# Down product of a 4-bit FFN: seven of eleven weight chunks as whole numbers in single passes

## Chip, cores, metric

The kernel runs on one core of one Trainium2 chip. The metric is the device time of one execution in microseconds; lower is better. A run of the kernel before is quoted by the median of three executions.

## The reference, cut to what matters

The program is four layers, each an attention and a feed-forward part (FFN). Only the first FFN (L0 FFN) is changed. It takes x of 4 x 256 = 1024 tokens by 512 features, three 4-bit weight matrices (gate and up 512 x 1376, down 1376 x 512), and computes down(silu(gate(x)) * up(x)). A weight is a whole number of 0 to 15 less a zero point, times a scale for each group of 128 input rows and each output column:

```python
def dequant_gptq(qweight, scales, zeros, groupsize):
    q = qweight[k // PACK, :] >> (k % PACK * 4)[:, None] & 15
    z = zeros[:, n // PACK] >> (n % PACK * 4)[None, :] & 15
    zp = (z.astype(jnp.float32) + 1.0) * s
    return q.astype(jnp.float32) * s[k // groupsize] - zp[k // groupsize]
```

So q - z - 1 is a whole number between -16 and 14, and within one group of 128 rows the scale can be taken out of the sum over rows. The 1376 rows of the down matrix are 11 chunks of 128 (the last one padded), and each chunk is exactly one group.

## The kernel before

All 1024 tokens are handled as 8 tiles of 128 (NT = 8), features as 4 chunks of 128 (NC = 4). Activations x_sb hold tokens on the partitions; xT holds features on the partitions. The order of every engine's instructions in the L0 FFN is the order in the source (`manual_schedule`); DMA instructions on SP's queue and everything outside this function are placed by the tile framework's scheduler. Each engine executes its own queue in order. Waits are set by the framework, by tile: an instruction waits for earlier users of the memory that it touches.

**Weights ahead of time.** `GateUp` (L596 on) works in the shadow of the attention: it fetches the packed words of gate and up, shifts out the nibbles (`nibble`), subtracts the zero points (`whole`, L666) and keeps whole numbers, for the first READY = 3 blocks as float32r and for eight more as float16. `points` (L620 on) forms the zero points of all three matrices; for down it forms scaled zero points and stores them to DRAM (`down_zp`).

**Gate and up** (`Sum`, L746 on; loop at L790). There are 22 sub-products: 11 blocks of 128 inner features, gate and up for each. x was split into a high half (float32r) and the rest (`hi`, `lo`), so that a product of x with whole-number weights takes two single-pass matmuls. Each sub-product is 4 groups x 2 token halves x 2 (hi, lo) = 16 matmuls into four PSUM tiles of two banks (F=4); ACT scales two of them out of PSUM (L776), DVE scales and adds the other two (L778), POOL adds the two sums (L783, `added`), ACT takes the Silu (L798) and DVE multiplies gate by up (L801) into hT, which holds inner features on the partitions: 11 chunks x 1024 tokens, float32. ACT also widens float16 weights to float32r (`widen`, L678).

**Down** (L816 on). `down_fetch` has SP fetch packed words, scales and scaled zero points of one chunk, mostly into xT, which is free by then; `down_weights` shifts the nibbles out on DVE (L718), multiplies by the scales on DVE (L722) and subtracts the scaled zero points on POOL (L723), giving float32 weights in `wd`. Chunks 0 and 1 are made during the last gate/up sub-products, the others during the product. `product` (L730) is one float32 matmul: 128 tokens of hT are the stationary side, the 512 weight columns move, and the result has tokens on the partitions. The loop first does chunks 0 to 4 for all eight token tiles, then chunks 5 to 10 for tiles 0 to 3; `output` copies the PSUM tile to float16 on ACT (L727) and adds it to x_sb on DVE (L728). While tiles 4 to 7 get chunks 5 to 10, layer 1's norm of tiles 0 to 3 runs in steps between them (statistics, L140 normalisation, L147 transposes, L906 queries).

**What lies around it.** `x2` is the pool that holds hi and lo; it is closed at L815, and layer 1's weights (`layer1_begun`: w1, rank, bqk, b1 by SP; gate_b and bv by POOL's queue) are loaded into its place. `values_binding` (L863 on) works on bv: seven DVE instructions (L867 to L852 of `signs`), a memset on POOL, and an ACT operation on bqk. `binding` needs that ACT result for a small matmul (L881). Layer 2's first weights (`Layer2Weights`, SP L91 and L1114, eight sums on POOL at L1095 and L1099) are loaded when the pools of the gate and up weights are given back, after the last `down_weights`. The `wd` buffer is also lent to the attention: output weights `wo` in chunks 0 to 3, attention outputs `oT` in chunks 4 to 9.

Of the kernel before, what the change touches and what calls it, by code (L numbers as in the profile page):

```python
# [23 lines left out]
I32 = mybir.dt.int32  # L24
# [16 lines left out]
ROWS = NBLK * P // PACK  # L41
READY = 3
# [13 lines left out]
def block_stack(ctx: ExitStack, tc: tile.TileContext, d: dict, out: bass.AP):  # L56
# [94 lines left out]
    def layer0_attention(hook, aside, xp, wd):  # L151
# [13 lines left out]
        with (  # L165
# [10 lines left out]
            wo = wd[:, 0:4, :]  # L176
# [82 lines left out]
            class Batch:  # L259


                def __init__(self, b):
# [3 lines left out]
                    k = 4 + 2 * (b % 3)  # L266
                    self.oT = wd[:, k : k + 2, :].rearrange("p c i -> p (c i)")
# [328 lines left out]
    class GateUp:  # L596
# [6 lines left out]
        def __init__(self, pool, raw, ready, held, dram):  # L603
            self.pool, self.raw, self.ready, self.held = pool, raw, ready, held
            self.built = {}

            self.z = dram.tile([2, 4, NBLK, P], F16, name="gu_z1")
            self.down_zp = dram.tile([NBLK, C], F32, name="down_zp")

        def load(self):  # L610
# [4 lines left out]
            ds = self.raw.tile([P, 4, P], F16, tag="z", name="ds_rows")  # L615
            self.ds = ds[0:NBLK].rearrange("p c i -> p (c i)")
            nc.sync.dma_start(out=self.ds, in_=d["down_s"])
            self.s = self.pool.tile([P, 2, NBLK, 4], F32, name="gu_s32")

        def points(self):  # L620
# [3 lines left out]
            dzi, zp = (self.raw.tile([P, 4, P], I32, tag="q", name=k) for k in ("d_zi", "d_zp"))  # L624
            dzi, zp = (x[0:NBLK].rearrange("p c i -> p (c i)") for x in (dzi, zp.bitcast(F32)))
# [8 lines left out]
            def finish():  # L634
# [4 lines left out]
                nc.vector.scalar_tensor_tensor(zp, dzi, 1.0, self.ds, ALU.add, ALU.mult)  # L639
                nc.sync.dma_start(out=self.down_zp, in_=zp)  # L640
# [3 lines left out]
        def pieces(self, blk):  # L644
            steps = []
            self.built[blk] = ws = []
            for m, name in enumerate(("gate", "up")):
# [13 lines left out]
                def whole(name=name, had=had):  # L661
                    if blk < READY:
                        w = self.ready.tile([P, 4, P], F32R, tag=name, name=f"{name}_w_{blk}")
                    else:
                        w = self.held.tile([P, 4, P], F16, name=f"{name}_h_{blk}")
# [15 lines left out]
    def layer0_ffn(gu, layer1_begun, x2, wd, hi, lo, outputs):  # L681
        E = mybir.EngineType
        with (
# [8 lines left out]
            spare = [xT[:, c, :].rearrange("p (k i) -> p k i", k=2) for c in range(NC)]  # L692
            fetched_down = {}

            def down_fetch(m, pool=None):

                if pool is not None:
                    q = pool.tile([P, C], I32, tag="dq", name=f"dq_{m}")
                    s = pool.tile([P, C], F16, tag="ds", name=f"ds_{m}")
                    zp = pool.tile([P, C], F32, tag="dzp", name=f"dzp_{m}")  # L700
                elif m != 6:
                    k = (m - 2) % 5
                    q, zp = spare[k][:, 0].bitcast(I32), spare[k][:, 1]
                    s = xT[:, NC - 1, k * 256 : (k + 1) * 256].bitcast(F16)
                else:
                    q = gu.raw.tile([P, 4, P], I32, tag="q", name=f"dq_{m}")
                    zp = gu.raw.tile([P, 4, P], F32, tag="q", name=f"dzp_{m}")
                    s = gu.raw.tile([P, 4, P], F16, tag="z", name=f"ds_{m}")
                    q, zp, s = (x.rearrange("p c i -> p (c i)") for x in (q, zp, s))
                nc.sync.dma_start(out=q, in_=bc(d["down_q"][:, m], 0, 8))  # L710
                nc.sync.dma_start(out=s, in_=bc(d["down_s"][m], 0, P))
                nc.sync.dma_start(out=zp, in_=bc(gu.down_zp[m], 0, P))
                fetched_down[m] = q, s, zp

            def down_weights(m):

                q, s, zp = fetched_down[m]
# [3 lines left out]
                w = wd[:, m, :]  # L721
                nc.vector.tensor_tensor(w, q, s, ALU.mult)  # L722
                nc.gpsimd.tensor_tensor(w, w, zp, ALU.subtract)  # L723
# [6 lines left out]
            def product(t, po, k):  # L730
# [3 lines left out]
                    rhs=wd[:, k, :],  # L734
                    start=k == 0,
                    stop=k == NBLK - 1,
                )

# [1536 lines left out]
```

## Time and profile before

| | us |
|---|---|
| median of 3 executions (lowest, highest) | 1412.58 (1407.13, 1414.27) |
| profiled execution, its own time | 1412.54 |
| span of the profiled execution | 1410.8 |
| first gate/up matmul | 275.27 |
| first and last down matmul (starts) | 369.35, 446.5 |
| first matmul of layer 1 (rank) | 447.80 |
| busy TensorE / DVE / ACT / POOL, share of span | 96% / 63% / 37% / 52% |

Times within the profile count from the start of the span. A matmul's record starts when it is issued, and the next begins before its end is reached; so the price of one in a row of many is the distance of starts, not the duration. The mean granted TensorE clock was 0.983 of full speed.

### The profile page before, as it was taken

The page shows a single profiled execution, that of the slowest core. Times are in us where ns is not written, and L with a number is a line of the kernel's source. Part 1 is how long each engine was busy: PE and PEld are TensorE (multiplying, and loading weights), DVE is VectorE, ACT ScalarE, POOL GpSimd, SP SyncE. Part 2 cuts the span into 40 slices and gives each one's busy share as a digit, 9 for nine tenths or more (in the row PEclk, how much of TensorE's full clock was granted, in tenths as well). Part 3 has the DMA queues.
Part 4 walks back from the last instruction along what each step waited for, and adds up shares of the span by engine and source line. Part 5 has one row for each costly group of instructions (what it writes and reads, how often), then busy time and mean ns, then how long its engine had stood idle before and what let it go on. Part 6 is the DMA issues. An engine that isn't in the chain of part 4 may idle for free.

```text
span 1410.8 us, 20812 instructions
## 1 busy us (share of the span) xinstructions
PE 1359.0 (96%) x7300; PEld 1068.8 (76%) x7300; DVE 895.8 (63%) x2366; ACT 520.7 (37%) x1337; POOL 734.1 (52%) x760
## 2 busy tenths in 40 slices
PE   7989999999999999999999999999999999989998
PEld 5656666578545667888888888888888888867887
DVE  6777878468927249635756756665566655858654
ACT  2343435378303212332333432333333344535430
POOL 3445546457743105864777857868558675210210
PEclk9889999899999999999999999999999999999999
DMA  5021212400420021011312203211123000302001
GB/s 195 2 58 35 47 35 63 111 0 1 140 80 16 0 80 48 31 46 34 98 45 64 68 16 94 68 46 64 53 60 105 22 25 1 135 1 112 0 1 60
DMA packets 50812, 76.15 MB, mean 54 GB/s; under 512 B 16476, under 2 KB 23799, under 8 KB 50323
## 3 DMA queue, kind: packets, MB, share of 16 engines
q1 hardware_dynamic: 49778, 73.77, 17.0%
q8 instruction: 58, 0.95, 0.3%
q10 hardware_dynamic: 816, 0.79, 0.2%
q14 instruction: 48, 0.39, 0.1%
q0 software_dynamic: 112, 0.26, 0.1%
HBM read 66.89 MB, written 7.91 MB: 53 GB/s over the span
## 4 chain that ended last, share of the span: by engine, by line
PE 84%; DVE 10%; ACT 2%; issue 1%; POOL 1%; DMA 1%; SPq 0%; DVEq 0%; ACTq 0%; POOLq 0%
PE m L1367 18%; PE m L1331 15%; PE dn L731 5%; PE gu L763 5%; PE s L1720 4%; PE av L1793 4%; PE m L1353 3%; PE m L1343 3%; PE half L278 3%; PE st L435 2%; PE s L1724 2%; PE av L1794 2%; PE l1o L1010 2%; DVE masked L389 2%; PE half L318 2%; PE half L343 1%
## 5 line engine op out<-in xcount | busy, mean ns | idle before, releaser
L1768 POOL TENSOR_TENSOR p<-p,rs 128x512 f32<-128x512 f32 (+1 forms) x128 | 107.7, 863 | 160.6 <-DVE rs L1765 148.9
L1754 ACT ACTIVATE p<-p,nm 128x256 f32<-128x256 f32 (+1 forms) x256 | 113.2, 443 | 108.2 <-DVE nm L1738 108.0
L1331 PE MATMUL m<-xT,wq_b 128*128 128x256 f32 x448 | 105.5, 384 | 4.4 <-DVE x_sb L1590 3.0
L1425 DVE TENSOR_TENSOR x_sb<-x_sb,m 128x512 f32<-128x512 f32 x82 | 55.9, 685 | 82.4 <-PE m L1367 67.4
L1738 DVE CUSTOM_DVE_ANT_0 p<-s,cmask 128x256 f32<-128x256 f32 (+1 forms) x256 | 76.1, 353 | 45.9 <-PE s L1720 43.8
L1391 POOL TENSOR_TENSOR q<-q,t 128x512 f32<-128x512 f32 x64 | 82.3, 1287 | 31.5 <-DVE t L1382 28.2
L389 DVE CUSTOM_DVE_ANT_0 masked<-s,cmask 128x256 f32<-128x256 f32 (+1 forms) x256 | 89.8, 351 | 11.7 <-PE s L376 2.0
L1802 ACT COPY o<-av 128x512 f32<-128x512 f32 x64 | 37.5, 586 | 157.7 <-PE av L1794 157.7
L1331 PEld LDWEIGHTS m<-xT,wq_b 128*128 128x128 f32 x448 | 83.2, 193 | 15.2 <-DVE x_sb L1590 3.4
L1314 POOL TENSOR_TENSOR c<-c,z 128x512 f32<-128x512 f32 x28 | 36.5, 1303 | 111.0 <-DVE c L1311 50.7
L449 POOL TENSOR_SCALAR_AFFINE_SELECT keys<-keys 128x256 f32<-128x256 f32 x128 | 57.0, 457 | 66.0 <-ACT keys L445 64.6
L1367 PE MATMUL m<-wo_b,o 128*128 128x256 f32 x384 | 89.6, 379 | 0.0
L1382 DVE TENSOR_TENSOR t<-m,rope_sb 64x512 f32<-64x512 f32 (+1 forms) x144 | 86.3, 599 | 2.1
L445 ACT ACTIVATE keys<-st 128x384 f32<-128x384 f32 x128 | 57.3, 488 | 78.1 <-PE st L435 78.1
L1786 ACT COPY q<-pT 128x512 f32<-128x512 f32 x64 | 37.5, 585 | 122.5 <-PE pT L1777 120.5
L731 PE MATMUL dn<-wd,hT 128*128 128x512 f32 x176 | 76.4, 593 | 2.3 <-DVE sb L778 2.3
L1367 PEld LDWEIGHTS m<-wo_b,o 128*128 128x128 f32 x384 | 71.3, 190 | 8.8
L783 POOL TENSOR_TENSOR sa<-sa,sb 128x1024 f32<-128x1024 f32 x22 | 62.0, 2822 | 30.5 <-DVE sb L778 30.5
L1331 PE MATMUL m<-x_s,wq_t 128*128 128x256 f32 x320 | 75.4, 380 | 1.2 <-ACT kv L1416 1.1
L1331 PEld LDWEIGHTS m<-x_s,wq_t 128*128 128x128 f32 x320 | 59.8, 190 | 10.1 <-ACT kv L1416 1.5
L1793 PE MATMUL av<-q,kv 128*128 128x512 f32 x128 | 65.5, 593 | 0.9 <-ACT q L1787 0.9
L1720 PE MATMUL s<-kv,q 128*128 128x256 f32 x256 | 65.8, 379 | 0.0
(328 smaller groups left out, 3423.8 us busy)
## 6 DMA issues: line engine op xcount, KB each, us to landing
wq_b<-in_wq SPq DMA_DIRECT2D x38, 256.0 KB
wo_b<-in_wo SPq DMA_DIRECT2D x32, 256.0 KB
raw<-in_wo SPq DMA_DIRECT2D x16, 512.0 KB
wkv_b<-in_wkv SPq DMA_DIRECT2D x16, 256.0 KB
wos_d<-wos_row SPq DMA_DIRECT2D x28, 128.0 KB
gate_q<-in_gate_q SPq DMA_DIRECT2D x11, 256.0 KB
up_q<-in_up_q SPq DMA_DIRECT2D x11, 256.0 KB
wq3s_b<-in_wq SPq DMA_DIRECT2D x8, 256.0 KB
```

Source lines behind the costliest of these rows:

```text
L389: nc.vector.tensor_tensor_reduce(out=ap.tile([P, T], F32, tag="masked", name="masked", bufs=1)[:, 0:n], in0=self.s[part][i][:, e, :], in1= ...
L731: nc.tensor.matmul(po, lhsT=hT[:, k, t * P : (t + 1) * P], rhs=wd[:, k, :], start=k == 0, stop=k == NBLK - 1,)
L763: nc.tensor.matmul(p[:, half], lhsT=w[:, g, :], rhs=x[half][:, g], start=k == 0, stop=k == 1,)
L1331: nc.tensor.matmul(out[:, i, :], lhsT=b[:, c, i * P : (i + 1) * P], rhs=a[:, c, :], start=start and i == 0 and c == 0, stop=i == 1 and c == 1,
L1367: nc.tensor.matmul(out[:, t, :], lhsT=a[:, c, t * P : (t + 1) * P], rhs=b[:, c, :], start=start and t == 0 and c == 0, stop=t == 1 and c = ...
L1382: nc.vector.tensor_tensor(t2[at], src[of], sin[of], ALU.mult)
L1391: after(1 + 2 * pause, lambda: nc.gpsimd.tensor_tensor(dst, dst, t2, ALU.add))
L1720: nc.tensor.matmul(s1[:, i, :], lhsT=q[:, i, P:T], rhs=kt[:, 0, :], start=True, stop=True)
L1738: nc.vector.tensor_tensor_reduce(out=x[f"p{part}"][:, e, :], in0=x[f"s{part}"][:, e, :], in1=cmask if part else cmask[:, P : 2 * P], scale ...
L1754: nc.scalar.activation(p, p, AF.Exp, bias=x["nm"][:, part, e : e + 1], scale=-1.0, accum_out=x["sums"][:, part, e : e + 1],)
L1768: nc.gpsimd.tensor_tensor(p, p, bc(x["rs"][:, part, :], 2, n), ALU.mult)
L1793: nc.tensor.matmul(av, lhsT=v[:, 0:P], rhs=x["q0"], start=True, stop=False)
```

## The change

The constant WHOLE = 7 divides the chunks of the down product.

Chunks 0 to 6 keep whole-number weights: `down_weights` shifts the nibbles out and subtracts the zero point (now q - (z + 1), float32r), and applies no scale. hT of these chunks is split into a float32r part (ACT) and the rest (POOL) by `split`. `whole` multiplies with the weights as the stationary side: 128 output columns on the partitions, 512 tokens moving, two token halves, two parts each, in single passes. A result (one chunk, 128 output columns, 1024 tokens) takes a PSUM tile of two banks; `scaled` multiplies it by the scale, which is now a value for each partition, and adds it to `acc` in SBUF: on DVE for three of four column blocks, and by ACT and POOL for the fourth. `turned_back` brings the sums into the output's layout with a float32 matmul against the identity, accumulating on top of the other chunks' result.

Chunks 7 to 10 stay as they were: scaled float32 weights (scale now multiplied on POOL) and `product`. Sixteen of these products (tiles 0 to 3) are placed before and between the 28 steps of the whole-number loop, the others in the second half as before.

Around this: PSUM is one pool of four two-bank tiles A to D through the whole FFN, and pairs of token tiles share one (dn_0 with dn_1, and so on); zero points of down are stored unscaled in DRAM and fetched in one broadcast; packed words of chunks 7 to 10 go straight into their weight buffers; `acc` takes the place of the float16 gate/up weights and the split parts take the places of gate/up weights (chunks 0 and 5) and of hi and lo (the others); x2 is closed after the loop, and `values_binding` follows it. The diff, cut to its core:

```diff
+WHOLE = 7
...
+            def down_tiles():
...
+                nc.sync.dma_start(out=points, in_=bc(gu.down_z1, 0, P))
+                nc.sync.dma_start(out=scales, in_=bc(d["down_s"][WHOLE:NBLK], 0, P))
+                for m in (0, 7, 1, 8, 9, 10):
+                    down_fetch(m)
...
             def down_weights(m):
-                q, s, zp = fetched_down[m]
+                w, q = wds[m], packed[m]
                 nc.vector.tensor_scalar(
                     q, q, gu.shift, 15, ALU.logical_shift_right, ALU.bitwise_and
                 )
-                w = wd[:, m, :]
-                nc.vector.tensor_tensor(w, q, s, ALU.mult)
-                nc.gpsimd.tensor_tensor(w, w, zp, ALU.subtract)
+                nc.vector.tensor_tensor(w, q, points[:, m, :], ALU.subtract)
+                if m >= WHOLE:
+                    nc.gpsimd.tensor_tensor(w, w, scales[:, m - WHOLE, :], ALU.mult)
+                elif m + 2 < WHOLE:
+                    down_fetch(m + 2)
+            def split(k, eng):
...
+                for i, h in enumerate(hs):
+                    nc.scalar.copy(x[2 * i], h)
+                for i, h in enumerate(hs):
+                    eng.tensor_tensor(x[2 * i + 1], h, x[2 * i].bitcast(F32), ALU.subtract)
+                halves[k] = x[:2], x[2:]
+            def whole(k, n, p):
+                for h in range(2):
+                    for i, x in enumerate(halves[k][h]):
+                        nc.tensor.matmul(
+                            p[:, h],
+                            lhsT=wds[k][:, n * P : (n + 1) * P],
+                            rhs=x,
+                            start=i == 0,
+                            stop=i == 1,
+                        )
+            def scaled(k, n, p):
+                s, a = gu.ds[:, n, k : k + 1], acc[:, n]
+                if k == 0 and n % 2 == 0:
+                    nc.scalar.activation(a, p, AF.Copy, scale=s)
+                elif k == 0:
+                    nc.vector.tensor_scalar(a, p, s, None, ALU.mult)
+                elif n == 3:
+                    part = once.tile([P, 2, 512], F32, tag="part", name=f"part_{k}")
+                    nc.scalar.activation(part, p, AF.Copy, scale=s)
+                    nc.gpsimd.tensor_tensor(a, a, part, ALU.add)
+                else:
+                    nc.vector.scalar_tensor_tensor(a, p, s, a, ALU.mult, ALU.add)
+            def turned_back(t, po):
+                for n in range(4):
+                    nc.tensor.matmul(
+                        po[:, n * P : (n + 1) * P],
+                        lhsT=acc[:, n, t // 4, t % 4 * P : (t % 4 + 1) * P],
+                        rhs=ident,
+                        start=False,
+                        stop=n == 3,
+                    )
...
+                    if u in (8, 12, 16, 20):
+                        down_weights({8: 0, 12: 7, 16: 1, 20: 8}[u])
+                    if u in (20, 21):
+                        split(u - 20, nc.gpsimd)
+                side = {
+                    2: [lambda: down_weights(2)],
+                    3: [lambda: split(2, nc.gpsimd)],
+                    4: [lambda: finish(len(subs) + 1)],
+                    5: [lambda: split(3, nc.gpsimd)],
+                    6: [lambda: down_weights(3)],
+                    8: [lambda: split(4, nc.gpsimd), lambda: down_weights(9)],
+                    11: [lambda: down_weights(4)],
+                    12: [lambda: split(5, nc.gpsimd)],
+                    14: [lambda: down_weights(10)],
+                    15: [lambda: down_weights(5)],
+                    17: [lambda: split(6, nc.gpsimd)],
+                    19: [lambda: down_weights(6)],
+                }
+                po = []
+                for _ in range(2):
+                    two = bank([P, 2, 512], f"dn_{len(po)}")
+                    po += [two[:, 0], two[:, 1]]
+                between = [(t, k) for k in range(WHOLE, NBLK) for t in range(4)]
+                for _ in range(4):
+                    t, k = between.pop(0)
+                    product(t, po[t], k)
+                finish(len(subs))
+                ring = turn[0] + 1
+                for i in range(4 * WHOLE):
+                    k, n = divmod(i, 4)
+                    p = ps("ABCD"[(ring + i % 2) % 4], [P, 2, 512], f"dw_{k}_{n}")
+                    whole(k, n, p)
+                    scaled(k, n, p)
+                    for f in side.get(i, ()):
+                        f()
+                    if i >= 4 and i % 2 == 0 and len(between) > 2:
+                        t, j = between.pop(0)
+                        product(t, po[t], j)
+                for t, k in between:
+                    product(t, po[t], k)
             x2.close()
-            ctx0.enter_context(psum_banks("ps_f1", F=4, G=4))
             l1 = layer1_begun()
-            po = [ps("FG"[t // 4], [P, C], f"dn_{t}") for t in range(NT)]
-            early, rest = range(NBLK // 2), range(NBLK // 2, NBLK)
-            for k in early:
-                if k >= 2:
-                    down_weights(k)
-                    down_fetch(k + 5)
-                for t in range(NT):
-                    product(t, po[t], k)
             l1.values_binding()
-            for k in rest:
...
             for t in range(4):
+                turned_back(t, po[t])
                 output(t, po[t])
-            steps = l1.norm(0, "F")
-            steps.insert(1, lambda: l1.binding("F"))
+            tags = ["ABCD"[(ring + i) % 4] for i in range(4)]
+            for i in range(2):
+                two = ps(tags[i], [P, 2, 512], f"dn_{len(po)}")
+                po += [two[:, 0], two[:, 1]]
+            steps = l1.norm(0, tags[2:])
+            steps.insert(1, lambda: l1.binding(tags[2]))
             for t in range(4, NT):
                 steps[t - 4]()
-                for k in rest:
+                for k in range(WHOLE, NBLK):
                     product(t, po[t], k)
+                turned_back(t, po[t])
                 output(t, po[t])
```

`finish(u)` holds what the gate/up loop did at L794 to L801 (the sum, the Silu, the multiplication of an earlier sub-product); its last two calls now stand in the down product.

## The prediction

> **What bounds the kernel now.** The mean clock is 0.983 and TensorE is busy for 96% of the span, so only a stretch in which TensorE does less, or waits, can move the time. First the chain of waits through the end of the feed-forward network, then busy time by stretch:
>
> ```profile
> 368.02 1.29 DVE sb L778
> 369.35 60.35 PE dn L731 x140
> 429.82 5.25 PE dn L731 x12
> 435.95 5.15 PE dn L731 x12
> 441.98 5.17 PE dn L731 x12
> 447.16 0.59 ACT o L727
> 447.80 3.80 PE rank L933 x32
> ...
> 288.00:367.00 79.00, 79.00 (x339) 62.96 (x337) 65.40 (x57) 64.50 (x69) 57.64 (x21) 1.00 0.04 9
> 367.00:447.00 80.00, 77.68 (x195) 35.24 (x194) 45.93 (x71) 8.12 (x13) 37.75 (x28) 1.00 0.29 89
> ```
>
> The columns of the last two are stretch, length, then busy time (instructions) of PE, PEld, DVE, ACT and POOL. The down product is a solid TensorE block with other engines half idle; gate and up before it are also TensorE-bound, at 3.74 us for one of 22 sub-products. I measure from the end of the last gate/up matmul (starts 366.64, takes 0.40: 367.04) to the first rank matmul (447.80): **80.76 us**. Prices, from the groups by line and by source:
>
> ```profile
> L731 PE MATMUL dn<-wd,hT x176: 592/592/697, 369.4 to 446.5; 128*128 128x512 f32 x176
> ...
> L783 POOL TENSOR_TENSOR sa<-sa,sb x22: 2341/2414/3381, 290.6 to 370.6; 128x1024 f32<-128x1024 f32 x22
> L778 DVE SCALAR_TENSOR_TENSOR sa<-gu,gu_s,sa x22: 1272/1284/1284, 288.0 to 366.8; 128x1024 f32<-128x1024 f32 x22
> L722 DVE TENSOR_TENSOR wd<-xT x6: 693/1636/1642, 375.6 to 392.6; 128x512 f32<-128x512 int32 x6
> L801 DVE TENSOR_TENSOR hT<-hT,sa x11: 1212/1216/2477, 301.7 to 373.9; 128x1024 f32<-128x1024 f32 x11
> bv<-in_bv POOLq DMA_DIRECT2D x1, 256.0 KB, 4.0
> ```
>
> Durations are minimum/median/maximum in ns. The 88 products of the source leave 176 records, 140 of them in 60.35 us: one product costs 2 x 0.431 = **0.862 us**. Gate/up matmuls (f32r) start every **0.2335 us** and leave one record. DVE's evacuation from PSUM starts every 1.20 us when queued; ACT's (L776) every 1.02.
>
> **What the Trainium skill says.** "FP8 and Floating Point Precision", TensorE Precision Notes: true FP32 makes four passes. The trace agrees: 0.862/0.2335 = 3.7. "SBUF — State Buffer", SBUF: two separate sides: a DVE operation with two SBUF inputs and a GpSimd one that reads SBUF exclude each other; the one that "starts first gets the pair for the whole instruction". The trace agrees: L722 takes 0.69 alone and 1.64 while L723 runs, L801 1.21 or 2.4, L783 2.41 or 3.33; L778, with one operand in PSUM, never varies. "DMA: Bandwidth & Descriptors", Anatomy of one DMA, fits a GpSimd-issued transfer at 2.0 us + bytes/436 KB per us: an estimate of 2.6 us for bv; the trace says 4.0, which I take, keeping 2.6 as the short end.
>
> **TensorE's own work.** Seven of eleven chunks leave the FP32 form: 7 x 8 x 0.862 = 48.3 us go. In come 7 chunks x 4 output blocks x 2 halves x 2 (high, low) = 112 single passes x 0.2335 = 26.2, and 8 x 4 turning matmuls of 128 columns at 0.22 (L1018: 8 records, 4 instructions, in 0.89) = 7.0. The change of PSUM pool at 366.6 to 369.35 goes too (2.3). Net -17.4 us, **if nothing waits**. Things wait.
>
> **The loop.** From 367.04, four FP32 products (chunk 7) run at once: 3.45. Then 28 steps of 0.934, ten products put between them (8.6): 34.8. All 28 steps share two two-bank buffers, so each waits for the evacuation two steps back, and DVE has other work between evacuations:
> - Start. POOL must first scale chunk 8 (1.3), split chunk 0 (2 x 1.24) and add sub-product 20 (2.36); it ends near 372.3. ACT stands at the Silu that needs this add (0.97), and the first evacuation is behind it. The third step starts near 374.5: a stall of 2.3, and 0.4 at the fifth.
> - The last hT multiply at step 4 (DVE, 2.3 with POOL ahead of it): 1.6 over two steps.
> - down_weights (0.5 + 0.62 alone, 1.55 beside POOL) at steps 2, 6, 8, 11, 14, 15, 19: 1.5 at step 8, 1.8 at the pair 14/15, 0.4 at 19, nothing where TensorE has a product to do.
> - Chunk 6 has no products between its steps: 0.934 against an evacuation of 1.28 gives about 1.0.
> Sum 9.0, and 0.1 for each of eleven restarts (first dn record after its idle time: 697 against 592 ns): 10.1. Loop: 3.45 + 34.8 + 10.1 = **48.3**, ending at 415.3 = T.
>
> DVE alone in it: 18 x 1.2 + 2 x 1.2 + 7 x 1.1 to 2.1 + 2.3 = 34 to 41. Bounds: no exclusion at all, loop 44.9 (-3.4); every exclusion against us, POOL at 1.4/2.8, loop 52.2 and 2.2 more in gate/up (+6).
>
> **The tail, where I expect the gain to go.** The split activations lie where layer 1's weights go, so w1, rank, bqk, gate_b and bv load only after the loop's last matmul (before: issued 368.7 to 375, under the product), and values_binding moves from the middle of the product to the front of the DVE queue after the loop. By the built order and its waits:
> - POOL: memset of lowT (1.2; before at 375.2), the last sum (2.4) to T+3.75, gate_b issue (0.7), bv issued at T+4.5, landed T+8.5.
> - DVE: values_binding, 4.4 us (380.38 to 384.80 before), T+8.5 to T+12.9. Behind it on the queue: the residual adds.
> - TensorE: two products, then tile 0's turning, whose fourth block waits for POOL's sum (1.5 stall), done T+4.1. Tile 1 shares a PSUM tile with tile 0 and waits for ACT's copy of tile 0; that copy stands behind the ACT operation waiting for bqk, third behind the 1 MB w1 (before: 7.3 us from issue to use), so T+9 to T+10.3: stall 6. Tile 3 waits for copy 2, which has two o16 buffers and so needs residual add 0: T+12.9 + 0.7 + 0.6 = T+14.4: stall 2.4. A shorter bqk only moves stall from the first to the second.
> - Tile 3 and tile 4 (4 x 0.862 + 0.88 = 4.33) end near T+20; tile 5 waits for copy 4, behind the square root of the statistics (adds to T+16.8, four statistics 3.1): stall 1.7. Tiles 5, 6, 7: 13.0 and sixteen transposes 1.8, T+36.6. Copy and handover 0.85: rank at **T+37.4**.
> With bv at 2.6, 1.4 less; at 6, 2 more.
>
> 48.3 + 37.4 = 85.7. The same bookkeeping over the kernel before gives 81.1 against 80.76 measured, so **+4.6**.
>
> **Moved at no cost, with the cover.** Two more down_weights, more scaling, and two splits fall into the gate/up stage, where DVE has 13.6, POOL 21 and ACT 14 us idle and four buffers cover; if that cover is gone, 0 to 2.2. Layer 2's first weights (SP, 394.8 to 399.9) and eight POOL sums (to 411.3) move to after the last turning, near 452; first use was 520.1, so some 50 us of cover remain. The sums now stand between layer 1's maskings: 5 us ahead of batch 0's last one, which still ends about 1.5 before its use. Without that margin: up to 2. The zero points become one 1.4 MB broadcast on SP at 263 (before: 0.25 MB), ahead of the up_q needed by DVE at 271.2. At the 239 GB/s seen in 369 to 385 it takes 6: 0 to 2 late, I take 0.5. ACT's split casts (10 x 0.6) lie in its idle loop time.
>
> Total +5.1. The profiled run took 1412.54 for a span of 1410.8, and the median is 1412.58, so both give **1417.6 us**.
>
> **Rivals.**
> (a) *The gain arrives*: the path ends on TensorE. For it: 17.4 us less TensorE work, and ACT idle. Against: bv cannot land before the loop ends. With the tail's waits gone (-10.5) but the loop's kept: 1407; all gone: 1395. Ends faster from about 12 us fewer waits than I count. 6%.
> (b) *DVE becomes the loop's bound* through the shared port: every two-input operation takes its long form. +14: 1426.5. It decides from 40 us of DVE work in the loop. 24%.
> (c) *Shorter waits*: bv in 2.6 us, half the exclusions: +1 to +2, 1414. 20%.
> (d) *My account*, 1414 to 1421: 50%.
>
> **Numbers.** A measurement of this kernel tells about 0.5% (7 us) from no change. (d) crosses +7 in about a quarter of its chance, (b) nearly always: slower 0.38; faster 0.05; within 0.57. Range 1410 to 1426: it leaves out most of (a) and the far half of (b).
>
> **What would show it.** Right: rank starts 3 to 8 us later relative to the last gate/up matmul; the waits list shows TensorE waiting at the turning matmul for ACT's o copy, 5 to 8 in total, and DVE waiting some 8 us for bv; turning matmuls at 0.22 an instruction; about 10 us of TensorE waits for DVE and ACT in the loop. Wrong: a turning stage without waits (then (a)), DVE at 90% through the loop (then (b)), gate/up longer than 3.74 a sub-product, or a later start of gate/up than 275.3.

## The result, and the profile after

The changed kernel takes **1421.21 us** (median of 13 runs, 1416.16 to 1425.87) against 1410.96 us (median of 13, 1403.19 to 1414.27): ratio **1.0076**, 95% interval 1.0058 to 1.0093, so some 10 us slower. Its profiled execution took 1417.51 us for a span of 1415.8 us, only 5 us more than the profiled one of before. What stands between 5 and 10 lies outside the three stages that the change touches. Ahead of the gate/up stage TensorE is granted half its clock for 23.9 to 47.8 us in the 14 traces of this case, and the first gate/up matmul starts anywhere from 270.0 us (with 23.9) to 277.6 us (with 47.8). So from here on I compare stages, which repeat: the gate/up stage (first gate/up matmul to the end of the last) takes 91.77 and 91.81 us in two executions of the old code, and 94.41 to 94.43 in seven of the new (the changed kernel and the experiments that leave the stage alone).

First, busy time by stretch. The columns are as before; the third figure from the right is the clock granted to TensorE. The first fence is the old gate/up stage, the second the new kernel's gate/up stage, loop and tail:

```profile
275.27:367.04 91.77, 90.15 (x384) 71.57 (x384) 67.64 (x62) 66.62 (x71) 58.04 (x22) 1.00 0.06 16
```

```profile
271.39:365.82 94.43, 91.85 (x385) 71.92 (x386) 74.32 (x66) 68.20 (x74) 59.27 (x23) 1.00 0.05 13
365.82:416.69 50.87, 43.60 (x141) 27.46 (x141) 42.33 (x38) 14.55 (x20) 40.34 (x24) 0.93 0.05 16
416.69:454.75 38.06, 30.10 (x119) 19.32 (x117) 21.04 (x50) 8.64 (x14) 10.60 (x9) 0.82 0.12 42
```

The sum of the three is 183.36 us; the old kernel has 91.77 + 80.76 = 172.53. That is **+10.8**: 2.65 in gate/up, 8.2 from the last gate/up matmul to the first rank matmul. The profiled spans show less of it because the new execution reached gate/up 3.9 us earlier (30.7 us at half clock before it, against 44.4), and because the old one was 1.95 us longer from rank to the end (963.0 us against 961.05), where it had a half-clock stretch at 1253 that the new one did not have. What the change moved behind the network cost nothing that can be seen there.

TensorE's waits in loop and tail, the new kernel's list (total, times, longest):

```profile
PE dn L803 <- ACT o L788: 5.3, 2, 2.8
PE dw L765 <- DVE gu_h L784: 3.9, 4, 2.0
PE dw L765 <- ACT gu_h L776: 2.9, 1, 2.9
PE dn L803 <- POOL gu_h L782: 1.4, 1, 1.4
PE rank L1040 <- ACT o L788: 0.7, 1, 0.7
PE dn L792 <- ACT o L788: 0.6, 1, 0.6
PE dw L765 <- ACT part L781: 0.3, 1, 0.3
```

It is the pattern that was forecast: the turning matmul (L803) waits for ACT's copy, the whole-number matmul (L765) for evacuations. The chain of work through the tail, where before there was one block of products:

```profile
418.05 2.35 POOL gu_h L782
421.03 3.67 DMA bv<-in_bv
424.84 0.70 DVE alpha_v L974
...
427.28 0.70 DVE v_hard L958
430.02 2.08 PE dn L803 x8
432.10 5.30 PE dn L792 x8
437.40 0.91 PE dn L803 x8
```

bv is issued after the last sum on GpSimd, lands, and VectorE's values_binding carries the chain on. But look at the last three lines: one tile's turning (`turned_back`: eight records, four instructions) takes 2.08 us at 430 and 0.91 at 437, and between them four products take 5.30 instead of 3.45. That is no wait. The clock granted up to 435.7 is half.

**The half clock.** The Trainium skill, "TensorE: Matmul & The Clock Gate", Part 1: The HAM clock gate, says that a gate passes half the clock after an idle window and all of it after a busy one, and that the window is free-running and 3413 ns long. The traces agree on the window: in the new kernel half-clock stretches begin at 46.60, 84.15, 166.07, 241.16, 251.40, 374.28, 391.35 and 422.07 us, which is, to a hundredth of a us, 0, 11, 35, 57, 60, 96, 101 and 110 windows of 3.4133 us. Cut along that grid, loop and tail read so:

```profile
370.87:374.28 3.41, 0.49 (x2) 0.29 (x2) 3.13 (x3) 2.06 (x2) 3.41 (x3) 1.00 0.00 0
374.28:377.70 3.42, 3.42 (x9) 2.63 (x9) 0.88 (x2) 1.83 (x3) 3.12 (x3) 0.50 0.15 53
387.95:391.36 3.41, 1.41 (x6) 0.67 (x4) 3.41 (x3) 0.00 (x0) 3.41 (x3) 1.00 0.01 2
391.36:394.77 3.41, 3.41 (x9) 2.16 (x7) 2.33 (x4) 2.14 (x3) 1.79 (x2) 0.50 0.12 36
418.67:422.08 3.41, 0.89 (x6) 0.51 (x4) 0.00 (x0) 0.00 (x0) 3.12 (x4) 1.00 0.88 323
422.08:425.49 3.41, 2.01 (x9) 2.01 (x10) 0.65 (x1) 0.68 (x2) 0.00 (x0) 0.50 0.24 78
```

A window in which TensorE is busy 0.49, 1.41 or 0.89 us is followed by one at 0.50. From 422.08 the half clock lasts four windows; TensorE is busy 2.01, 1.77, 2.30 and 3.41 us in them, so only the fourth is full. The kernel before has none of this between 260 and 1252 us.

### The profile page after: what moved, and what is told of

It reads as the page before. It is cut to its first block, busy times and chain, and to the rows that moved or that the text cites. A ratio compares the mean times of both kernels' runs of the same rounds, so it can differ in the third digit from the quotient of the medians.

```text
span 1415.8 us, 20980 instructions
## 1 busy us (share of the span) xinstructions
PE 1350.0 (95%) x7364; PEld 1078.2 (76%) x7364; DVE 922.1 (65%) x2387; ACT 536.6 (38%) x1359; POOL 758.7 (54%) x773
## 4 chain that ended last, share of the span: by engine, by line
PE 82%; DVE 13%; ACT 2%; DMA 2%; issue 1%; POOL 1%; SPq 0%; DVEq 0%; ACTq 0%; POOLq 0%
PE m L1474 18%; PE m L1438 15%; PE gu L839 6%; PE s L1827 4%; PE av L1900 4%; PE m L1460 3%; PE half L279 3%; PE m L1450 3%; DVE masked L390 2%; PE s L1831 2%; PE av L1901 2%; PE l1o L1117 2%; PE st L436 2%; PE half L319 2%; PE half L344 2%; PE dn L792 1%
## 5 line engine op out<-in xcount | busy, mean ns | idle before, releaser
L859 POOL TENSOR_TENSOR sa<-sa,sb 128x1024 f32<-128x1024 f32 x22 | 63.0, 2866 | 31.5 <-DVE sb L854 31.5
L1438 PEld LDWEIGHTS m<-x_s,wq_t 128*128 128x128 f32 x320 | 59.9, 190 | 10.1 <-ACT kv L1523 1.5
L1474 PE MATMUL m<-wo_t,o_s 128*128 128x256 f32 x256 | 59.2, 379 | 0.0
```

Of the source, the lines that this page charges most:

```text
L859: nc.gpsimd.tensor_tensor(self.a, self.a, self.b, ALU.add)
L1438: nc.tensor.matmul(out[:, i, :], lhsT=b[:, c, i * P : (i + 1) * P], rhs=a[:, c, :], start=start and i == 0 and c == 0, stop=i == 1 and c == 1,
L1474: nc.tensor.matmul(out[:, t, :], lhsT=a[:, c, t * P : (t + 1) * P], rhs=b[:, c, :], start=start and t == 0 and c == 0, stop=t == 1 and c = ...
```

## The experiments

All start from the changed kernel, but for one. A build is one call of `down_weights` (nibble operation, subtraction, and GpSimd's scaling for chunks 7 to 10); an evacuation is an operation that takes a result out of PSUM. "Stage" is gate/up, "loop" the end of the last gate/up matmul to the end of the last whole-number matmul (L765), "tail" from there to the first rank matmul, all in us and read from each trace; ratios are to the kernel before in runs beside it.

| kernel | stage | loop | tail | median | ratio (95%) |
|---|---|---|---|---|---|
| before | 91.77 | 80.76 in all | | 1410.96 | 1 |
| changed | 94.43 | 50.87 | 38.06 | 1421.21 | 1.0076 (1.0058 to 1.0093) |
| turn_first | 94.42 | 51.63 | 36.19 | 1421.10 | 1.0076 (1.0055 to 1.0096) |
| early_bv | 94.42 | 51.64 | 31.53 | 1417.42 | 1.0040 (1.0023 to 1.0056) |
| awake | 94.42 | 50.98 | 35.71 | 1418.22 | 1.0045 (1.0026 to 1.0063) |
| gate_order | 97.91 | 52.99 | 37.06 | 1427.31 | 1.0109 (1.0086 to 1.0132) |
| silu_late | 94.42 | 50.80 | 38.27 | 1422.30 | 1.0064 (1.0039 to 1.0088) |
| light | 94.41 | 49.80 | 36.97 | 1423.00 | 1.0075 (1.0055 to 1.0095) |
| joint | 94.42 | 46.77 | 36.93 | 1416.23 | 1.0040 (1.0021 to 1.0058) |
| combo1 | 97.91 | 53.77 | 30.27 | 1422.27 | 1.0070 (1.0053 to 1.0087) |
| combo2 | 105.78 | 42.69 | 30.16 | 1418.29 | 1.0048 (1.0033 to 1.0064) |
| combo3 | 99.31 | 46.60 | 26.31 | 1406.59 | 0.9976 (0.9957 to 0.9995) |
| combo4 | 93.03 | 50.19 | 26.31 | 1408.36 | 0.9987 (0.9969 to 1.0005) |

### The tail: turn_first and early_bv

```
             for t in range(4):
                 turned_back(t, po[t])
+            for t in range(4):
                 output(t, po[t])
```

> The four turnings stand ahead of the four copies and adds of the first half; nothing else differs from the changed kernel. Theory A (the loss is TensorE's waits, plus the half clock that follows the long ones): the two waits of the turning matmul for ACT's copy (2.5 and 2.8 us) go, the four turnings end some 5.5 us after the last whole-number matmul, and one wait of about 5 us appears at tile 5's products, set by the chain bv, values_binding, residual adds, copies; loop end to rank shrinks from 38.1 to 31-35 us, time 3 to 7 us below the changed kernel, 0.2 to 0.5% above the kernel before. Rival B (VectorE bounds the loop and the tail's waits are covered anyway): tail within 1 us of 38.1. Rival C (the throttle costs the time, wherever the waits are): the half-rate time after the loop stays about 13.6 us and the gain is under 2 us.

The two waits at L803 went, as expected, and one of 7.3 us came at tile 5's products; the tail shrank by 1.9 only, not by 3 to 7, and the median did not move. So the order of TensorE's own work was not what set the tail's end. The chain bv, values_binding, residual adds, copies was left, and early_bv shortens that chain itself:

```
+            def binding_weights():        # called at sub-product 8
+                gu.bqk = load(fp, "bqk")
+                gu.bv = fp.tile([P, L1_HEADS, P], F32, name="bv")
+                nc.sync.dma_start(out=gu.bv, in_=bc(d["bv"], 0, P))
```

> bqk and bv are loaded on SP in the gate/up stage into memory of their own; orders of TensorE, ACT and VectorE as in the changed kernel. Theory A: VectorE no longer waits 8.2 us for bv nor ACT 4.8 us for bqk; values_binding runs 1 to 5 us after the last whole-number matmul; of TensorE's waits in the tail about 1.4 (POOL's last sum), 1 at tile 1, 1 at tile 3 and 0.6 at tile 5 are left, no half-rate period after the loop; loop end to rank 29 to 32 us instead of 38.1, time 6 to 9 us below the changed kernel, about level with the kernel before. Rival B: within 1 us of the changed kernel. Rival C (half clock from elsewhere): waits go but a half-rate period of 3.4 us or more still lies behind the loop, gain 3 to 5.

Tail 31.5, 6.5 less, inside the forecast; the loop came out 0.8 longer, and the time gained 3.8 us of the 6 to 9 expected. VectorE's wait for bv, which the first line below shows for the changed kernel, is gone from its list. The other two lines are early_bv's:

```profile
DVE alpha_v L974 <- DMA bv<-in_bv: 8.2, 1, 8.2
```

```profile
423.27:426.68 3.41, 1.36 (x10) 0.98 (x9) 3.34 (x3) 0.59 (x1) 2.86 (x3) 1.00 0.92 354
426.68:430.10 3.42, 3.42 (x16) 3.14 (x15) 2.31 (x4) 0.59 (x1) 0.00 (x0) 0.50 0.05 3
```

One half-clock window was left, where theory A expected none. So the tail's length fits theory A, and rival C had the rest right, the window and the gain of 3 to 5: with the waits cut to 1.4 us (GpSimd's sum), 1.4 (two of ACT's copies together) and 1.0, one window was still busy for 1.36 us only.

### The half clock: gaps and awake

gaps is the kernel *before* with idle times of known length in its solid product:

```
                 for t in range(NT):
+                    if t == 4:
+                        for _ in range(k + 1):
+                            nc.scalar.copy(wd[:, k, :], wd[:, k, :])
                     product(t, po[t], k)
```

> The kernel before, with five idle times of TensorE put into its down product: in the middle of each of the first five chunks ACT copies that chunk's weights onto themselves 1, 2, 3, 4 and 5 times (0.58 us each), and the next products wait for it. Theory A: idle times of about 0.9, 1.5, 2.1, 2.7 and 3.2 us; the longer three are followed by a stretch of 3.4 us at half the clock (products starting every 1.7 us instead of 0.862), the first not; each such stretch costs 1.7 us. Total about +10 us of idle and +3 to +7 us of half clock: 1425 to 1430. Rival (the half clock is not set off by idle time): no half-rate stretch in the down product, +10 us, 1422.

1426.73 us in its one run, inside theory A's range (the rival's was 1422), with two half-clock stretches in the down product, where the kernel before has none. The idle times came out at 0.71, 1.36, 2.06, 2.71 and 3.36 us. The windows (the same grid, counted from the first half-clock stretch of this execution) around the last three, in pairs of window and successor:

```profile
389.93:393.34 3.41, 1.35 (x4) 0.68 (x4) 3.34 (x5) 1.85 (x3) 2.16 (x3) 1.00 0.50 132
393.34:396.76 3.42, 3.42 (x5) 1.35 (x4) 3.38 (x3) 0.00 (x0) 2.45 (x2) 0.50 0.06 17
400.17:403.58 3.41, 0.73 (x2) 0.00 (x0) 0.00 (x0) 2.47 (x4) 1.90 (x2) 1.00 0.92 318
403.58:407.00 3.42, 3.39 (x4) 1.51 (x5) 0.00 (x0) 0.00 (x0) 3.42 (x4) 0.50 0.30 113
410.41:413.82 3.41, 2.00 (x5) 0.57 (x3) 0.00 (x0) 1.25 (x3) 1.26 (x2) 1.00 0.00 0
413.82:417.23 3.41, 1.46 (x4) 0.74 (x5) 0.00 (x0) 1.95 (x4) 0.00 (x0) 1.00 0.00 0
```

Idle 2.06 and 2.71 each lay within one window and halved the next. The **longest, 3.36 us, halved nothing**: it fell across a border, leaving 2.00 and 1.46 us of work on either side. My expectation "the longer three" was wrong in that; length is not the measure, the share of a window is. That also fits the kernel before, whose 2.32 us idle time at the change of pools leaves 1.61 us in its window. Over all 14 traces, from 300 us on, no full-clock window with less than 1.46 us of work kept the clock, and none with more than 1.78 lost it; between these two figures both happen. At half clock no window under 3.13 regained it. The page speaks of an idle window; here about half a window was enough. The figures hold for this part of the program only: ahead of 300 us, in the attention, windows that the profile shows busy for as much as 3.03 us were followed by half clock too (in the new kernel the one from 237.75), so busy time in the profile is not all that counts.

awake fills the four longest waits with products of zeros:

```
+                    for _ in range({2: 2, 11: 2}.get(i, 0)):
+                        idle_product(po[3])              # lhsT all zero, 0.86 us each
...
+                for _ in range({1: 2, 3: 4}.get(t, 0)):
+                    idle_product(po[4], True)
                 turned_back(t, po[t])
```

> Waits are left as they are; into four of them idle products with an all-zero operand are put (two ahead of the third and the twelfth whole-number step, two ahead of tile 1's turning, four ahead of tile 3's), 0.86 us each, 8.6 us of added TensorE work. They add nothing to the sums. Theory A (an idle time of 2 us or more is followed by 3.4 us or more at half the clock): the three half-rate stretches (3.4, 3.4 and 13.6 us) go or shrink to at most one, matmuls after these places start every 0.2335 us again, and the time falls by 4 to 6 us although TensorE has 8.6 us more to do. Rival (waits alone; the half clock is no consequence of the idle time): half-rate stretches as before and 0 to 3 us slower.

```profile
371.99:422.97 50.98, 45.93 (x150) 27.79 (x149) 43.19 (x38) 14.57 (x20) 40.29 (x24) 0.97 0.06 16
422.97:458.68 35.71, 30.75 (x131) 18.07 (x129) 21.82 (x50) 8.53 (x14) 10.60 (x9) 1.00 0.13 45
```

20.5 us of half clock became one window, in the loop (408.32). The tail lost 2.35 us although it has six idle products more, with bv issued and landed as before. The median lies 3 us lower, but the two intervals overlap. So in the tail the half clock was on the path, and useless work bought time. **The loop did not move at all** (50.98 against 50.87), with one half-clock window in place of two and four idle products more. So the half clock alone did not set its length. Of theory A's 4 to 6 us about half came.

### The loop: silu_late, light, joint

silu_late issues the last sum and the Silu that waits on it after the second step, so that ACT's first evacuation is free; light leaves the five builds of weights out of the loop:

```
-                finish(len(subs))
                 side = {
+                    1: [lambda: finish(len(subs))],
```

> Only the loop's start is touched: the last sum on GpSimd and the Silu on ACT that waits for the sum before it are issued after the second whole-number step instead of ahead of the first, so that ACT's first evacuation is not queued behind them. Theory A (the first wait of 2.9 us and the half clock after it are on the path): that wait falls under 0.6 us, the half-rate stretch after it goes, and the loop falls from 50.9 to 46.5-48.5 us. Rival B (VectorE's work sets the loop's end, and TensorE's waits and half clock only fill its slack): the wait is found again at later steps and the loop stays at 50 to 51.

```
-                    2: [lambda: down_weights(2)],        # and those of 3, 4, 5, 6
+                wds.update({m: wds[m % 2] for m in range(2, WHOLE)})
```

> Leaves out part of the computation: the weights of down chunks 2 to 6 are not built, their steps use those of chunks 0 and 1 (10 VectorE operations and five transfers less in the loop, all else as in the changed kernel). Theory A (single late evacuations): the waits at steps 8, 14, 15 and 19 go, the start's stays, loop 50.9 to about 47. Rival B (VectorE bounds the loop): the loop shrinks by what the ten operations took, 0.5 and 0.7 to 1.64 each, 7 to 9 us, to 42-44, where TensorE's own 38.3 and the start's wait begin to bound it.

Each did what it was to do and gained next to nothing: loop 50.80 and 49.80. In silu_late the first wait of 2.9 became 0.3, and the wait for VectorE grew:

```profile
PE dw L765 <- DVE gu_h L784: 6.4, 5, 2.4
PE dn L803 <- ACT o L788: 5.3, 2, 2.9
```

In light, which leaves out part of the computation, VectorE itself stood idle ahead of its evacuations (last figures: idle time and what ended it), so it was not the bound once its load was gone:

```profile
L782 DVE SCALAR_TENSOR_TENSOR gu_h<-dw,down_s,gu_h 128x1024 f32<-128x1024 f32 x17 | 21.3, 1279 | 8.6 <-PE dw L763 8.2 <-ACT x_hi L754 0.3
```

Rival B as I wrote it (VectorE alone, 42 to 44) fell, and so did theory A. Two bounds of nearly equal length would give this, and joint, both edits in one (so it too leaves the builds out), tests it:

> silu_late and light in one: the start without ACT's queue, and (this leaves out part of the computation) the weights of chunks 2 to 6 not built. Each alone moved the loop by 0.1 and 1.1 us. Theory E (two bounds of nearly equal length, the start's and step 12's waits with their half-clock stretches on one side, VectorE's work with the port losses on the other; taking one away leaves the other): together the loop falls to 43-46 us. Rival F (something third holds the loop at 50, GpSimd's sums for instance): 49 or more.

46.77: **0.1 and 1.1 us apart, 4.1 us together**. It ended just above the 43 to 46 expected, with the twelfth step's wait of 2.0 us and one half-clock window (392.13) still in it; rival F, a third bound at 49 or more, fell.

### The shared port: gate_order and the four combinations

Where do the 2.65 us of gate/up come from? The new kernel's timeline at its first build of weights:

```profile
316.43 0.48 DVE L731 TENSOR_SCALAR dq<-dq,shift_sb 128x512 int32<-128x512 int32 x1
316.60 2.58 POOL L859 TENSOR_TENSOR sa<-sa,sb 128x1024 f32<-128x1024 f32 x1 [0.42 <-DVE sb L854]
316.95 2.78 DVE L734 TENSOR_TENSOR wd<-dq,xT 128x512 fp32r<-128x512 int32 x1
319.65 1.27 DVE L854 SCALAR_TENSOR_TENSOR sa<-gu,gu_s,sa 128x1024 f32<-128x1024 f32 x1
...
320.98 0.50 PE L839 MATMUL gu<-x_hi,gate_w 128*128 128x512 f32 x1 [0.48 <-DVE sa L854]
```

The subtraction L734, 0.69 us alone, takes 2.1 us more beside GpSimd's sum: the SBUF port that the two engines share is held (the lock that the prediction quotes). The evacuation behind it on VectorE comes late, and TensorE stops. It happens twice, and by the distances of matmul starts it costs 1.0 us each time; the rest of the 2.65 is spread over smaller delays. gate_order put the nibble operation ahead of the two evacuations, so that the subtraction would come first:

> Only the gate/up stage is touched: in the four sub-products that build down weights the nibble operation is issued ahead of the two evacuations, so that the subtraction of the points directly follows them on VectorE and starts before GpSimd's sum does. Theory D (two subtractions that lose the shared port, 2.78 us instead of 0.69, make the evacuation late and cost the stage 2.65 us): both subtractions take 0.7 us, TensorE's two waits of 0.5 us in the stage go, the stage falls from 94.4 to 91.8-92.4 us and the loop and tail stay within 0.5 us; 2 to 3 us below the changed kernel. Rival (VectorE simply has too much to do there, whatever the order): stage 94 or longer, no change.

The stage got 3.5 us worse. Two reasons, both in the trace. The nibble operation itself lost the port:

```profile
312.31 3.32 POOL L862 TENSOR_TENSOR sa<-sa,sb 128x1024 f32<-128x1024 f32 x1 [1.35 <-DVE sb L857]
313.28 2.63 DVE L729 TENSOR_SCALAR dq<-dq,shift_sb 128x512 int32<-128x512 int32 x1
...
317.16 0.50 PE L842 MATMUL gu<-x_hi,up_w 128*128 128x512 f32 x1 [0.96 <-DVE sa L857]
```

It has one SBUF tensor input only, and I had counted it at 0.5 us throughout. The Trainium skill, "SBUF — State Buffer", SBUF: two separate sides, names a VectorE operation "in a 2-port perf mode" beside one with two SBUF inputs; 0.48 us became 2.63 here, which agrees with it, and my reading of that sentence was too narrow. Second, the edit placed GpSimd's scaling of chunks 7 and 8 ahead of the sum of the sub-product before, and ACT waited for that sum: TensorE then waited for ACT, 2.5 us in the stage and 1.7 just behind it. The subtraction itself took 0.68 us in this order, so theory D was right about it; my order moved the loss elsewhere.

combo1 joins gate_order, silu_late, early_bv and the 16 turnings block by block:

> The changed kernel with the order of gate_order, the start of silu_late, bqk and bv loaded early as in early_bv, and the 16 turning matmuls of the first half block by block over the four tiles ahead of the four copies. If the parts add: gate/up -2.5, tail -8 (two waits of 0.7, one of 1.4 and a half-rate stretch less than early_bv), loop 0 (rival B) to -3 (theory A): 1407 to 1411, level with the kernel before or up to 0.3% faster. If the waits only move: 1413 to 1416.

Tail 30.3, 7.8 less, as expected; stage and loop are 3.5 and 2.9 longer, as in gate_order. The time, 1422, lies above even the case that the waits only move. combo2 builds seven chunks in the stage, nibbles between the evacuations of an odd sub-product, subtraction right behind those of the next, and puts the products of tiles 4 and 5 ahead of their turnings:

> Nothing left out. Gate/up stage: seven instead of four chunks of down weights are built there, the nibble operation between the two evacuations of an odd sub-product and the subtraction right behind the two of the next even one, where GpSimd holds no port. Loop: start as in silu_late, four builds instead of seven. Tail: bqk and bv early, turnings of the first half block by block ahead of the copies, products of tiles 4 and 5 ahead of their turnings. Theory D+E (port losses by order, loop with two bounds, tail by loads and queues): the stage takes 91.8 to 92.5 us although it does more, loop 42 to 45, tail 27 to 28.5; 1400 to 1404 us, 0.5 to 0.8% faster than the kernel before. Rival (VectorE and GpSimd have too much to do in the stage): stage 94 or more, loop as expected, 1404 to 1408.

Loop 42.7 as forecast, tail 30.2 instead of 27 to 28.5, stage 105.8 instead of 92: the same misplaced scaling, now four times (TensorE waited 9.4 us for ACT in the stage). The theory's number failed there; the rival's "94 or more" covers the stage, but not the time, which it put at 1404 to 1408. The short loop may in part be a gift of the long stage, in which the other engines could get ahead; no run shows how much. combo3 issues the scaling behind the sum:

```
                     if u in AHEAD:
                         down_points(AHEAD[u])
                     finish(u)
+                    if u in AHEAD:
+                        down_rest(AHEAD[u])      # GpSimd's scaling
```

> combo2 with two queue places mended: GpSimd's scaling of a down chunk is issued behind the sum of the sub-product before it, not ahead of it (in combo2 that sum, ACT's second buffer and TensorE stood 9.4 and 2.4 us behind it), and the binding's matmul and sign operations stand ahead of tile 4's products (in combo2 the transposes waited 3.1 us for them). Theory: a build costs VectorE 1.2 us and nobody else anything as long as nibbles and subtraction fall where GpSimd holds no port and no sum is queued behind; then the stage takes 91.8 to 93 us with seven builds, loop 42.5 to 44, tail 27 to 28: 9 to 11 us less than the kernel before, 0.991 to 0.994. Rival (seven builds are too much for the stage): stage 95 to 98, 0.996 to 1.0.

Tail 26.31, with no wait over 0.8 us in it, and a stage 6.5 shorter than combo2's: the two mended places paid. But the loop took 46.6 instead of 42.5 to 44, the stage 99.3, beyond even the rival's 95 to 98, and the ratio is the rival's. The nibble operation two sub-products after a scaling meets GpSimd's delayed sum each time:

```profile
333.03 1.18 POOL L744 TENSOR_TENSOR wd<-wd,xT 128x512 f32<-128x512 f32 x1 [0.79 <-DVE wd L739]
334.16 2.39 POOL L876 TENSOR_TENSOR sa<-sa,sb 128x1024 f32<-128x1024 f32 x1
334.21 2.63 DVE L734 TENSOR_SCALAR wd<-wd,shift_sb 128x512 int32<-128x512 int32 x1
...
338.09 0.51 PE L854 MATMUL gu<-x_hi,gate_w 128*128 128x512 f32 x1 [1.45 <-DVE sb L869]
```

Still it is the first version whose interval lies below the kernel before, by 0.05 to 0.43%. The stages do not carry that: they sum to 172.22 us, 0.3 below 172.53, where the median is 5.5 lower. Eleven executions took 1399.31 to 1403.66 us and eleven 1409.52 to 1413.69, so the median of 1406.59 stands where none was, while of the 27 of the kernel before only five took less than 1406. So most of this gain seems to be a larger share of short executions; why it was larger is open. combo4 leaves a free place after each scaling and puts six builds back into the loop:

> combo3 with the builds placed by what its trace shows. In the gate/up stage five (0, 1, 2 without a GpSimd operation; 7 and 8 with one, each followed by a free even sub-product, since in combo3 every nibble operation two sub-products after a GpSimd scaling stood 2.1 us behind GpSimd's sum and TensorE waited 1.4). The other six in the loop, nibbles and subtraction put behind different steps instead of together. Theory: stage 91.8 to 93 us (99.3 in combo3), loop 44 to 48 (46.6), tail 26.3 as in combo3: 7 to 10 us less than the kernel before in the same state of the clock ahead of the stage, ratio 0.993 to 0.996. Rival (the port losses only move to other operations): stage 94 or more, loop 49 or more, ratio 0.998 to 1.001.

```profile
273.62:366.65 93.03, 91.27 (x385) 72.00 (x386) 73.89 (x68) 68.01 (x73) 61.73 (x25) 1.00 0.07 18
366.65:416.84 50.19, 42.16 (x142) 25.09 (x141) 44.72 (x36) 15.28 (x21) 38.34 (x22) 1.00 0.03 11
416.84:443.15 26.31, 24.87 (x119) 15.87 (x117) 24.69 (x51) 8.31 (x14) 9.64 (x8) 1.00 0.18 55
```

The stage came as forecast, with five builds and no wait for VectorE's evacuations: it does more than the changed kernel's and is 1.4 us shorter, so at least that part of the 2.65 was due to the order and not to the amount of VectorE's work. There is no half clock in any of the three. The loop took 50.2 all the same, in the rival's "49 or more": eight waits for VectorE, 7.4 us, VectorE busy 44.7 of it. So, read from its waits, with the six builds and the port losses in it the loop is VectorE's, as rival B of silu_late had it. The three sum to 169.5, 3.0 below the kernel before, of 7 to 10 expected; the median is 3.2 lower than that of the runs beside it (1411.51), but the interval includes 1, where the rival had it.

## Why the prediction was right, and where it was not

The time lay in the range (1410 to 1426, forecast 1417.6, measured 1421.2), and the 17.4 us of TensorE's work that went were eaten up in the places that were named, the loop's start and steps and the tail. But the rise was 10 us and not 5, and at 0.76% it lies past the 0.5% that I could tell apart: "slower", which I gave 0.38 against 0.57 for "same". Step by step:

- **TensorE's own work**: right. Whole-number matmuls start every 0.2335 us, turnings take 0.22 an instruction, products 0.862.
- **Gate/up "at no cost, with the cover"**: the step that failed outright. I gave 0.5 for the broadcast of the zero points and said that four buffers cover the two extra builds. The broadcast cost nothing seen (in the traces with 44.4 us of half clock ahead, the old kernel starts gate/up at 275.3 and 275.9, the new one at 275.5 to 275.9), the builds cost **2.65**, by the shared port. "0 to 2.2 if that cover is gone" was too small as well, and a sub-product longer than 3.74 us, named as a sign of being wrong, was there.
- **Waits of the loop**, 9.0: measured 7.1. The start was 2.9 (2.3 + 0.4), the build put behind step 8 cost 2.0, felt at the twelfth step (1.5), the pair 1.3 (1.8), the hT multiply 0.3 instead of 1.6.
- **The tail**: the chain was right in place and order. bv landed 8.0 us after the loop (8.5), values_binding took 3.85 (4.4). bqk was in use 5.1 us after issue, not 7.3, so tile 1 waited 2.5 and not 6; tile 3 2.8 (2.4), tile 5 0.6 (1.7). With POOL's sum and the handover, 8.0 us of waits for 12.4 forecast.
- **"0.1 for each of eleven restarts"**: the mis-sized term. It knew no half clock, although the mean clock of 0.983 in the table of the kernel before was a sign that there is one; "only a stretch in which TensorE does less, or waits, can move the time" left it out. During the busy time of those stretches TensorE lost half: 3.4 us in the loop, some 4.7 in the tail (3.78 and 5.70 us busy). Restarts proper take what is left, some 3.1 (88.93 less 62.6 of work, 15.1 of waits, 8.1 of clock).

So loop and tail came out 3.2 over (50.87 + 38.06 against 85.7) from waits 6.3 too high and a clock and restarts 10.1 too low, the rest being rounding of the work. That two errors of this size hid each other was luck. The bookkeeping is not yet causation: in awake the loop keeps its length with one half-clock window less, and in combo4 it takes 50.2 us with none. Shown are 2.35 us of the clock in the tail, 6.5 of bv and bqk's late loads there, and for the loop that two bounds stand side by side (joint).

Of the rivals, (b) had the mechanism in part: in the new loop the seven nibble operations took 3.8 + 1.9 = 5.7 us instead of 7 x 0.48, and the seven subtractions 5.3 + 2.3 = 7.6 instead of 7 x 0.69, together 5.1 us lost to the port. That is 1.9 us a chunk, near the upper end of the 1.1 to 2.1 of my own account. VectorE's 42.3 us of busy time passed the 40 from which (b) was to decide, and stayed under the 90% of the loop that was to show it (83%). VectorE alone did not set that loop (light). The larger group of each operation:

```profile
L734 DVE TENSOR_TENSOR wd<-dq,xT 128x512 fp32r<-128x512 int32 x5 | 5.3, 1051 | 0.2
L731 DVE TENSOR_SCALAR dq<-dq,shift_sb 128x512 int32<-128x512 int32 x5 | 3.8, 757 | 0.0
```

What stays open: how the loop's 50 us would fall with the port losses alone gone (no version without them was tried), why the page's "idle window" is here about half a window, and what else than the profile's busy time counts ahead of 300 us.

## What to carry to other kernels

Taking work off the engine that bounds a stage exposes whatever was hidden under it: here the loads tied to released memory, and the queues of three other engines. Price those first, one by one, and then in pairs, since two bounds of one length answer to no single edit. Where TensorE is left waiting, count not only the wait but the window it empties, and fill it with useful (or even idle) products if it can't be removed and TensorE ends the stage; that paid in the tail and not in the loop.

## What the hardware showed unexpectedly

- Half-clock stretches of TensorE begin on a grid of 3.413 us in all 14 traces, and which idle time sets one off depends on its place in the grid: 2.00 us did (busy 1.41), 3.36 across a border did not (busy 2.00 and 1.46). With nearly the same code ahead of it, gate/up started 7.6 us apart, with 23.9 and 47.8 us of half clock.
- Products of zeros on TensorE shortened the tail by 2.35 us.
- A nibble extraction with a single SBUF tensor input took 0.48 or 2.63 us, by whether GpSimd held the port.
